# A cross-attention kernel on one core: an order planned from both ends, and a set-up laid out anew

## The chip, the cores and the metric

The kernel runs on one core of one Trainium2 chip. The metric is the time of one execution on the device in microseconds (us), as a median of several runs. TensorE (PE) multiplies matrices, VectorE (DVE), ScalarE (ACT) and GpSimd (POOL) work elementwise, and SyncE (SP) issues DMAs, which ACT and POOL can do as well.

## What is computed

32 samples of x and of a context y, each of 256 channels by 1024 positions, in float32. For each sample:

```python
x_q = jnp.einsum('oc,bcn->bno', w_qk, y)
x_k = jnp.einsum('oc,bcn->bon', w_qk, x)
x_v = jnp.einsum('oc,bcn->bon', w_v, x) + b_v[None, :, None]
energy = jnp.einsum('bnc,bcm->bnm', x_q, x_k)
attention = jax.nn.softmax(energy, axis=-1)
attention = attention / (1e-07 + attention.sum(axis=1, keepdims=True))
x_r = jnp.einsum('bcn,bnm->bcm', x_v, attention)
x_r = jax.nn.relu(jnp.einsum('oc,bcn->bon', w_t, x - x_r) + b_t[None, :, None])
return x + x_r
```

So each sample has a 1024 by 1024 energy, a softmax over its rows, a division by the sums of its columns, and products with small weights before and after.

## The kernel before

**Three forms.** To multiply float32 values fast, each operand is kept as three forms (high, rest, low), and each product is the sum of three. `load_y` (L277) and `load_x` (L308) make the forms of y and x: ACT casts the high one, POOL or an accumulating DMA makes the other two. The weights are folded first: `gw` from w_qk squared, `vw` from w_t and w_v, `tw` from w_t transposed.

**Work of a sample.** Tokens name it: `k` the keys gf = gw x (`keys`, L363), `v`/`V` the values uf, `W` the straight product tw x, whose evictions ACT writes to xe with a bias, `E0` to `E7` eight row tiles of 128 rows of the energy (`energy`, L402), `A0` to `A7` their products with the values (`attention`), `S` the column sums, `O` the finish, `X`/`Y` the loads of x and y for what comes next. A `^` takes one of two upper pairs of PSUM banks (`high_pair`, L771), which alternate, 3 first; the others take a lower pair. `A` writes pair 2 for channels c=0 and pair 3 for c=1, so `O` has to read both before the upper pairs serve again.

**A row tile.** After the 12 products of a tile, DVE takes the row minimum, ACT the exponential, DVE a reciprocal, ACT writes the high form of each half, DVE the rest form and then adds the half to the column sums `acc`. All of these read the tile's two banks, and the tile that is next to use them waits until the last one is through. ACT and POOL make the low form.

**Who sets the order.** Every operation is first registered with the planner (`Plan`, L17) with an engine, a duration, a lag and the names that it reads and writes. PE keeps the order of the tokens (strings at L124 to L138: SET_UP, FIRST for sample 0, STEADY, BEFORE, LAST). `Plan.order` (L60) gives each operation a due time, counted back from its followers without regard to how busy the engines are, and then runs a list schedule: an engine that comes free takes the operation with the earliest due time among those that can start within a small look-ahead. `emit` (L113) tries three look-aheads, and the order with the shortest planned span is written out. For the planner an operation that reads a bank waits for readers of it on other engines that are registered ahead of it. On the chip each engine then runs its own list strictly in that order, waiting for data by semaphore. The planner lets a DVE operation whose operands lie in SBUF (`dve_in_sbuf`, L206) wait for a POOL operation that has begun; it makes POOL wait only behind such a wait.

**Set-up.** Loads go out on SP and ACT (L606 to L616): two of w_qk, four of x's first sample, one each of w_t and w_v, then y, b_v (spread over 128 partitions) and b_t on SP. `first_x` (L663) makes the first forms of x in four pieces (two halves of 512 columns, two channel blocks k): of six products of forms that DVE and POOL make, POOL makes the rest form of k=1, DVE that of k=0 and all four low ones. `first_keys` (L693) multiplies a form by gw, four products of a token being two; token `fL10` is the low form of k=1, half 0. `turn_w` transposes w_t; ACT copies it to wtT, and POOL makes the first step (`twd`) of its low form. `biases` (L736) multiplies w_t by b_v on DVE, sums it and makes three small biases. `load_y(0, direct=True)` lets POOL subtract y's high form from y in one piece of 1024 columns per partition; an accumulating DMA adds that to the low form.

Of the kernel before, what the change touches and what calls it, by code (L numbers as in the profile page):

```python
# [9 lines left out]
F32 = mybir.dt.float32  # L10
# [6 lines left out]
class Plan:  # L17
# [7 lines left out]
    SEEN = 0.1  # L25

# [33 lines left out]
    def order(self):  # L60
        ops = self.ops
        behind, before, last = {}, {}, None
        for op in ops:
            op.feeds = []
        for op in ops:
            for other in op.needs.values():
                other.feeds.append(op)
            if op.engine == "pe":
                if last is not None:
                    behind[last.at], before[op.at] = op, last  # L70
                last = op
        for op in reversed(ops):
            due = [f.due - op.busy - op.lag - self.SEEN for f in op.feeds]
            if op.at in behind:
                due.append(behind[op.at].due - op.busy)
            op.due = min(due, default=0.0) - op.early
        left = [len(op.needs) + (op.at in before) for op in ops]
        can = [0.0] * len(ops)
        free, ready, held, out = {}, {}, 0.0, []
        for op in ops:  # L80
# [3 lines left out]
        while len(out) < len(ops):  # L84
# [18 lines left out]
            if op.at in behind:  # L103
                nexts.append((behind[op.at], t + busy))
# [8 lines left out]
    def emit(self):  # L113
# [13 lines left out]
FIRST = (  # L127
    "V0^ W0^ V1 E0 E1^ W1 E2 E3 A0 A1 E4 E5 A2 A3 E6 E7 S X A4 A5 k0 Y2 A6 k1 A7 v0 Y3 O"
# [13 lines left out]
def kernel(  # L142
# [29 lines left out]
    Y_ON_POOL = False  # L172
# [83 lines left out]
    wtb = one.tile([P, KC], F32, name="wtb")  # L256
# [20 lines left out]
    def load_y(q, direct=False):  # L277
# [3 lines left out]
        name = {j: f"yf{s}{j}" for j in ORDER}  # L281
        from_ = y[b].rearrange("(k p) n -> p k n", p=P)[:, :, ts(half, MB)]
        by_sync(7.0 if b else 3.5, ["xr01", "xr11"] if b == 0 else [], ["yr"], lambda: sync.dma_start(r, from_))
        on_act(N, ["yr"], [name[HIGH]], lambda: act.copy(f[:, HIGH], r))
        if direct:
            on_pool(
                N, ["yr", name[HIGH]], [name[REST]],
                lambda: pool.tensor_tensor(f[:, REST], r, value(f[:, HIGH]), ALU.subtract),
            )
        else:  # L290
            on_act(N, [name[HIGH]], [name[REST]], lambda: act.mul(f[:, REST], value(f[:, HIGH]), -1.0))
            by_pool(9.0, [name[REST]], [name[REST]], lambda: accumulate(f[:, REST], from_))
        on_act(N, [name[HIGH]], [name[LOW]], lambda: act.mul(f[:, LOW], value(f[:, HIGH]), 1.0 / UP))
        if direct and q == 0 and Y_ON_POOL:
            on_pool(
                N, [name[LOW], name[REST]], [name[LOW]],
                lambda: pool.tensor_tensor(f[:, LOW], value(f[:, LOW]), value(f[:, REST]), ALU.add),
            )
        else:
            by_pool(  # L300
                8.0, [name[LOW], name[REST]], [name[LOW]],
                lambda: accumulate(value(f[:, LOW]), value(f[:, REST])),
            )
# [546 lines left out]
```

## Time and profile before

| | us |
|---|---|
| median of 3 runs (1948.5 to 1950.74) | 1948.7 |
| the profiled execution's own time | 1950.96 |
| its span, first to last instruction | 1949.2 |
| PE busy | 1938.1 (99%) |
| DVE busy | 1553.4 (80%) |
| ACT busy | 1434.6 (74%) |
| POOL busy | 1252.9 (64%) |

The span is what the profiler saw between the first and the last instruction; the execution's own time has 1.76 us around it. A line of the profile names the engine, the operation, the tile written and those read, the shape, and in brackets the idle time before it with what ended it. All operations go through one helper, so their line number is L188 throughout, and the tiles tell them apart.

### The profile page before, as it was taken

Reading aid. Unit: us, or ns where it says so; the run is one execution under the profiler, and the core shown is the slowest. Engines: PE = TensorE matmul, PEld = TensorE weight load, DVE = VectorE, ACT = ScalarE, POOL = GpSimd, SP = SyncE. Lnnn points to the kernel's source line nnn. Section 1 sums busy time; section 2 is a strip of 40 time slices with the busy share of each in tenths; the row PEclk is TensorE's granted clock in tenths of the full one; section 3 lists DMA queues with packets and bytes.
Section 4 is the critical chain, followed back from the end, with each engine's and each line's share of the span. In section 5 each row is a group of like instructions: output and inputs, shape, how many; then the busy total and the mean of one; then the engine's idle time right before and its main releaser. Section 6 shows DMA issues by size and latency. Waiting matters only on the chain.

```text
span 1949.2 us, 25297 instructions
## 1 busy us (share of the span) xinstructions
PE 1938.1 (99%) x9252; PEld 1632.4 (84%) x9252; DVE 1553.4 (80%) x2173; ACT 1434.6 (74%) x1863; POOL 1252.9 (64%) x645
## 2 busy tenths in 40 slices
PE   8999999999999999999999999999999999999998
PEld 7888888888888888888888888888888888888887
DVE  7887887877887778878788887887877887778887
ACT  6678776787767877667877678776787767877765
POOL 4577665766656666566766577665766656666564
PEclk9999999999999999999999999999999999999999
DMA  5545545564455554455544555545564445554540
GB/s 145 123 119 141 125 112 110 120 149 121 115 103 129 140 129 118 110 126 124 139 118 106 125 119 141 125 111 110 119 150 121 115 103 129 141 125 121 111 98 33
DMA packets 82140, 234.81 MB, mean 120 GB/s; under 512 B 7521, under 2 KB 8673, under 8 KB 82017
## 3 DMA queue, kind: packets, MB, share of 16 engines
q0 software_dynamic: 35280, 99.10, 29.7%
q1 hardware_dynamic: 46032, 133.19, 20.3%
q8 instruction: 73, 1.20, 0.2%
q10 hardware_dynamic: 704, 0.92, 0.1%
q14 instruction: 51, 0.41, 0.1%
HBM read 133.56 MB, written 33.55 MB: 86 GB/s over the span
## 4 chain that ended last, share of the span: by engine, by line
PE 98%; DVE 1%; ACT 0%; DMA 0%; issue 0%; POOL 0%; ACTq 0%
PE banks L188 98%; DVE xf L188 0%; DMA xr<-in_x_dram 0%; DVE ef L188 0%; DVE acc L188 0%; ACT xf L188 0%; ACT ef L188 0%; DVE z L188 0%; ACT banks L188 0%; DVE small L188 0%; POOL xf L188 0%; ACT xe L188 0%; DVE banks L188 0%; ACTq L188 0%; DVE gw L188 0%
## 5 line engine op out<-in xcount | busy, mean ns | idle before, releaser
L188 POOL TENSOR_TENSOR ef<-ef 128x1024 fp32r<-128x1024 f32 x256 | 614.6, 2407 | 442.2 <-ACT ef L188 229.4
L188 PE MATMUL banks<-gf,yf 128*128 128x512 f32 x3072 | 727.9, 389 | 0.4 <-DVE acc L188 0.4
L188 PE MATMUL banks<-ef,uf 128*128 128x512 f32 x3072 | 722.5, 389 | 1.2 <-DVE acc L188 1.2
L188 PEld LDWEIGHTS banks<-ef,uf 128*128 128x128 f32 x3072 | 576.5, 188 | 121.6 <-DVE acc L188 1.1
L188 PEld LDWEIGHTS banks<-gf,yf 128*128 128x128 f32 x3072 | 574.3, 188 | 119.5 <-ACT ef L188 0.8
L188 DVE SCALAR_TENSOR_TENSOR ef<-banks,small,ef 128x512 fp32r<-128x512 f32 x512 | 379.1, 746 | 149.5 <-ACT ef L188 149.2
L188 DVE TENSOR_REDUCE small<-banks 128x1 f32<-128x1024 f32 x256 | 312.6, 1221 | 102.7 <-PE banks L188 100.7
L188 ACT ACTIVATE banks<-banks,small 128x1024 f32<-128x1024 f32 x256 | 276.7, 1081 | 138.8 <-DVE small L188 138.1
L188 ACT ACTIVATE ef<-banks,small 128x512 fp32r<-128x512 f32 x512 | 320.7, 690 | 38.2 <-DVE small L188 38.2
L188 DVE SCALAR_TENSOR_TENSOR acc<-banks,small,acc 128x512 f32<-128x512 f32 x448 | 329.9, 742 | 0.0
L188 POOL TENSOR_TENSOR z<-z,xe 128x1024 f32<-128x1024 f32 (+1 forms) x64 | 151.3, 2381 | 205.0 <-DVE z L188 205.0
L188 ACT ACTIVATE ef<-ef 128x1024 fp32r<-128x1024 f32 x256 | 268.9, 1069 | 12.8 <-ACT ef L188 0.7
L188 ACT ACTIVATE gf<-banks 128x1024 fp32r<-128x1024 f32 x64 | 65.1, 1019 | 184.8 <-PE banks L188 184.7
L188 PEld LDWEIGHTS banks<-vw,xf 128*128 128x128 f32 x1536 | 193.8, 193 | 5.0
L188 PE MATMUL banks<-vw,xf 128*128 128x256 f32 x1536 | 195.2, 284 | 0.0
L188 PE MATMUL banks<-xf,gw 128*128 128x512 f32 x768 | 186.4, 391 | 4.0 <-DVE xf L188 2.3
L188 PE MATMUL banks<-xf,tw 128*128 128x512 f32 (+1 forms) x774 | 185.8, 389 | 0.8 <-DVE z L188 0.6
L188 PEld LDWEIGHTS banks<-xf,gw 128*128 128x128 f32 x768 | 143.9, 188 | 35.3 <-DVE xf L188 3.2
L188 PEld LDWEIGHTS banks<-xf,tw 128*128 128x128 f32 x774 | 142.5, 188 | 29.5 <-DVE z L188 0.8
L188 POOL TENSOR_TENSOR z<-z,xo 128x1024 f32<-128x1024 f32 x62 | 158.3, 2553 | 4.7 <-ACT ef L188 4.6
L188 POOL TENSOR_TENSOR xf<-xr,xf 128x1024 fp32r<-128x1024 f32 (+1 forms) x64 | 151.0, 2381 | 7.3 <-DVE xf L188 6.1
L188 DVE RECIPROCAL small<-small 128x1 f32<-128x1 f32 x256 | 41.1, 161 | 116.1 <-ACT banks L188 114.8
(65 smaller groups left out, 1403.7 us busy)
## 6 DMA issues: line engine op xcount, KB each, us to landing
yr<-in_ctx_dram SPq DMA_DIRECT2D x64, 512.0 KB, 3.7
yf<-yf POOLq DMA_DIRECT2D x64, 512.0 KB, 4.6
yf<-in_ctx_dram POOLq DMA_DIRECT2D x63, 512.0 KB, 6.7
xo<-in_x_dram SPq DMA_DIRECT2D x62, 512.0 KB, 4.5
xr<-in_x_dram SPq DMA_DIRECT2D x62, 512.0 KB, 3.4
xf<-xf POOLq DMA_DIRECT2D x62, 512.0 KB, 6.5
out_dram<-z SPq DMA_DIRECT2D x62, 512.0 KB, 5.0
out_dram<-z SPq DMA_DIRECT2D x3, 256.0 KB, 2.1
```

The lines of the kernel that those rows point to most:

```text
L188: self.last = getattr(self.engine, name)(*args, **kwargs)
```

## The change

- **The planner.** Due times of the first turn are counted as before. In three further turns they come from a second list schedule that runs from the end to the start and gives every engine one operation at a time, the later start of the turn before going first; the forward schedule then runs again. An engine takes what can start now, unless something more urgent becomes ready while that would run and is later than PE's own lateness allows; then it waits for that one. Of the four orders the one with the shortest planned span is written out.
- **Loads.** The planned landings are new (x 6.0 and 7.4 us where they were 3.8 and 5.0, for instance). w_t and w_v are loaded in two halves each, one on SP and one on ACT; ten loads now stand ahead of y, b_v and b_t.
- **Value bias.** w_t times b_v becomes four products of one column on PE (token `b`, ahead of `fR11` and `Q`), written to a corner of bank 7. DVE keeps the three small operations. b_v is now loaded as two columns in 4-byte pieces, as b_t is.
- **y's first forms in two pieces.** For the first half of y the first 256 positions (512 columns per partition) get both the rest and the low form on POOL; the other 256 positions get theirs by accumulating DMAs, as all later y do.
- **Column sums** are registered ahead of the high form of the same half, in every tile; for the planner ACT's high form then comes behind DVE's sum.
- **Token order.** SET_UP and FIRST are new; STEADY, BEFORE and LAST stay. FIRST has four `^` tokens where it had three.

```diff
--- before.py
+++ after.py
+    LOOKS = (0.0, 0.3, -0.6, 0.0)
...
+    def from_the_end(self):
+        left = [len(op.feeds) + (op.next is not None) for op in self.ops]
...
+        while todo:
...
+            op = max((o for o in ready[engine] if can[o.at] <= now), key=lambda o: (o.start, o.at))
+            ready[engine].remove(op)
+            todo -= 1
+            free[engine] = over = now + op.busy
+            op.due = -over - op.early
...
+        behind = -min(op.due for op in ops)
...
-            within = start + self.LOOK
-            op = min((o for o in ready[engine] if can[o.at] <= within), key=lambda o: (o.due, o.at))
+            op = min((o for o in ready[engine] if can[o.at] <= start), key=lambda o: (o.due, o.at))
+            late = start + op.busy - behind - self.LOOK
+            soon = [o for o in ready[engine] if can[o.at] < start + op.busy and o.due < min(op.due, late)]
+            if soon:
+                op = min(soon, key=lambda o: (o.due, o.at))
...
+            if engine == "pe":
+                behind = t - op.due
...
+    def best(self):
+        self.link()
         best = None
-        for look in (0.0, 0.15, 0.3):
-            self.LOOK = look
+        for turn, self.LOOK in enumerate(self.LOOKS):
+            if turn:
+                self.from_the_end()
             out = self.order()
             if best is None or self.span < best[0]:
-                best = self.span, out
-        self.span, out = best
-        for op in out:
+                best = self.span, [(op, op.start) for op in out]
+        return best
+
...
 SET_UP = (
-    "G x0 fH10 b fH00 fR10 x1 T fH01 fL10 Q fH11 y fR01 fL01 fL00 fR00 fL11 fR11"
+    "x0 G fR10 x1 fH10 T fR01 y fL10 fL00 fH00 b fR11 Q fL11 fR00 fL01 fH11 fH01"
 )
 FIRST = (
-    "V0^ W0^ V1 E0 E1^ W1 E2 E3 A0 A1 E4 E5 A2 A3 E6 E7 S X A4 A5 k0 Y2 A6 k1 A7 v0 Y3 O"
+    "V1^ V0^ W1 E0 E1^ W0^ X E2 E3 A0 A1 E4 E5 A2 Y2 A3 E6 E7 A4 A5 k0 k1 A6 S A7 Y3 O v0"
 )
...
-    def load_y(q, direct=False):
+    NQ = 2
+    QB = MB // NQ
+
...
+        by_sync(7.0 if q else 7.8, [], ["yr"], lambda: sync.dma_start(r, from_))
+        on_act(N, ["yr"], y_names(s, HIGH), lambda: act.copy(f[:, HIGH], r))
...
+            if q == 0 and which[0] == 0:
+                on_pool(
+                    columns, ["yr"] + nh, nr,
+                    lambda: pool.tensor_tensor(third, r[:, :, at], value(high), ALU.subtract),
+                )
+                on_act(columns, nh, nl, lambda: act.mul(low, value(high), 1.0 / UP))
+                on_pool(columns, nl + nr, nl, lambda: pool.tensor_tensor(low, value(low), value(third), ALU.add))
+                return
+            on_act(columns, nh, nr, lambda: act.mul(third, value(high), -1.0))
+            by_pool(9.0, nr, nr, lambda: accumulate(third, from_[:, :, at]))
+            on_act(columns, nh, nl, lambda: act.mul(low, value(high), 1.0 / UP))
+            by_pool(8.0, nl + nr, nl, lambda: accumulate(value(low), value(third)))
+
+        for which in ([0], [1]) if q == 0 else ([0, 1],):
+            pieces(which)
...
-            on_pe(KC, MB, [f"yf{s}{j}"] + [f"gf{j}{k}" for k in range(KC)], [at[h]], of)
+            on_pe(KC, MB, [f"yf{s}{j}{n % HT * NQ // HT}"] + [f"gf{j}{k}" for k in range(KC)], [at[h]], of)
...
         def halves(h):
             ph, to, a = both[:, h], f[:, :, ts(h, MB)], acc[:, ts(h, MB)]
             high, rest = names[HIGH][h], names[REST][h]
+            if n == 0:
+                on_dve(MB, [at[h], nm[2]], [f"acc{h}"], lambda: dve.tensor_scalar(a, ph, ri, None, ALU.mult))
+            else:
+                on_dve(
+                    MB, [at[h], nm[2], f"acc{h}"], [f"acc{h}"],
+                    lambda: dve.scalar_tensor_tensor(a, ph, ri, a, ALU.mult, ALU.add),
+                )
             on_act(MB, [at[h], nm[2]], [high], lambda: act.mul(to[:, HIGH], ph, ri))
             on_dve(
                 MB, [at[h], nm[2], high], [rest],
@@ -429,13 +484,6 @@
                     to[:, REST], ph, ri, value(to[:, HIGH]), ALU.mult, ALU.subtract
                 ),
             )
...
-    bv = two(3)[:, 1]
+    bv = two(3)[:, 0, P + KC : P + 2 * KC].rearrange("p (k o) -> p k o", o=1)
...
-    by_sync(5.6, [], ["wt"], lambda: sync.dma_start(wt, w_t.rearrange("(k p) c -> p k c", p=P)), early=25.0)
-    by_act(5.6, [], ["wv"], lambda: act.dma_start(wv, w_v.rearrange("(k p) c -> p k c", p=P)), early=25.0)
+    load(["wqk0", "wqk1"], 2.7, [(wqk[:, k], w_qk[ts(k, P)]) for k in range(KC)])
+    load(["xr00", "xr10"], 6.0, [(xr[:, k, half[0]], x[0, ts(k, P), half[0]]) for k in range(KC)])
+    load(["xr01", "xr11"], 7.4, [(xr[:, k, half[1]], x[0, ts(k, P), half[1]]) for k in range(KC)])
+    load(["wt0", "wt1"], 8.3, [(wt[:, k], w_t[ts(k, P)]) for k in range(KC)])
+    load(["wv0", "wv1"], 9.2, [(wv[:, k], w_v[ts(k, P)]) for k in range(KC)])
...
     def biases():
-        by_sync(4.0, ["xr01", "xr11"], ["bv"], lambda: sync.dma_start(bv, b_v.rearrange("(o c) -> o c", o=1).to_broadcast([P, C])))
-        by_sync(4.0, ["xr01", "xr11"], ["bt"], lambda: sync.dma_start(bt, b_t.rearrange("(k p o) -> p k o", p=P, o=1)))
-        product = work[:, N + KC * C :].rearrange("p (k c) -> p k c", k=KC)
+        by_sync(6.8, [], ["bv"], lambda: sync.dma_start(bv, b_v.rearrange("(k p o) -> p k o", p=P, o=1)))
+        by_sync(6.8, [], ["bt"], lambda: sync.dma_start(bt, b_t.rearrange("(k p o) -> p k o", p=P, o=1)))
+        wtb = banks[:, 7, C : C + KC]
+
+        def product():
+            for i in range(KC):
+                for k in range(KC):
+                    matmul(
+                        wtb[:, i : i + 1], wtT[:, k * C + i * P : k * C + (i + 1) * P], bv[:, k], k == 0, k == KC - 1
+                    )
+
+        plan.add("pe", 0.45, 0.163, ["wtT", "bv", "z1", "acc0", "acc1"], ["wtb", "bank7"], product)
 
         def of():
-            dve.tensor_tensor(product, wt, bv.unsqueeze(1).to_broadcast([P, KC, C]), ALU.mult)
-            dve.tensor_reduce(wtb, product, AX.X, ALU.add)
             dve.tensor_scalar(ubias[:, :, 0], wtb, EPS, None, ALU.mult)
-            dve.tensor_tensor(xbias[:, :, 0], bt[:, :, 0], wtb, ALU.subtract)
-            dve.tensor_scalar(nbias[:, :, 0], xbias[:, :, 0], -1.0, None, ALU.mult)
-
-        plan.add("dve", 2.0, 0.0, ["wt", "bv", "bt", "z1", "xe1"], ["bias"], of)
+            dve.tensor_tensor(nbias[:, :, 0], wtb, bt[:, :, 0], ALU.subtract)
+            dve.tensor_scalar(xbias[:, :, 0], nbias[:, :, 0], -1.0, None, ALU.mult)
+
+        plan.add("dve", 0.6, 0.0, ["wtb", "bank7", "bt", "z1"], ["bias"], of)
...
-            load_y(0, direct=True)
+            load_y(0)
             load_y(1)
```

## Rows read from the trace of the kernel before

**Rows 1.** The page: span, and each engine's busy time, share, instructions.
```profile
span 1949.2 us, 25297 instructions
...
PE 1938.1 (99%) x9252; PEld 1632.4 (84%) x9252; DVE 1553.4 (80%) x2173; ACT 1434.6 (74%) x1863; POOL 1252.9 (64%) x645
```
**Rows 2.** Busy time by stretch: stretch, its us, engines' busy us, TensorE's granted clock, DMA.
```profile
0.00:16.56 16.56, 11.46 (x47) 8.52 (x47) 9.62 (x13) 7.73 (x13) 8.61 (x12) 1.00 0.46 150
16.56:48.44 31.88, 31.49 (x152) 26.46 (x153) 25.47 (x37) 24.36 (x33) 13.46 (x8) 0.95 0.56 140
18.02:21.40 3.38, 3.38 (x15) 3.13 (x14) 3.28 (x8) 2.66 (x4) 1.59 (x1) 0.50 0.99 263
...
100.00:1880.00 1780.00, 1780.00 (x8505) 1501.47 (x8504) 1419.26 (x1983) 1331.38 (x1724) 1166.93 (x595) 1.00 0.52 123
1898.60:1906.40 7.80, 6.64 (x29) 4.67 (x27) 7.76 (x13) 6.83 (x10) 5.36 (x3) 1.00 0.26 106
```
**Rows 3.** PE's waits, whole run: waiter, releaser, total us, times, longest.
```profile
PE banks L188 <- DVE xf L188: 2.3, 2, 2.0
...
PE banks L188 <- DVE acc L188: 1.5, 3, 0.8
```
**Rows 4.** Timeline of PE, set-up and first sample: start us, us, what, idle before.
```profile
9.29 0.61 PE L188 MATMUL banks<-z 128*128 128x128 f32 x4
...
16.56 2.58 PE L188 MATMUL banks<-xf,gw 128*128 128x512 f32 x8 [2.03 <-DVE xf L188]
18.93 4.14 PE L188 MATMUL banks<-vw,xf 128*128 128x256 f32 x24
...
25.65 3.04 PE L188 MATMUL banks<-vw,xf 128*128 128x256 f32 x24
...
28.52 5.63 PE L188 MATMUL banks<-gf,yf 128*128 128x512 f32 x24
```
**Rows 5.** Timeline of DVE in the set-up.
```profile
9.68 1.78 DVE L188 TENSOR_TENSOR xf<-xr,xf 128x512 fp32r<-128x512 f32 x1
11.38 0.41 DVE L188 SCALAR_TENSOR_TENSOR gw<-banks,gw 128x256 fp32r<-128x256 f32 x1
...
13.06 4.04 DVE L188 SCALAR_TENSOR_TENSOR xf<-xf 128x512 fp32r<-128x512 f32 x3
...
18.60 0.68 DVE L188 TENSOR_TENSOR xe<-z 128x512 f32<-128x512 f32 x1
19.31 0.69 DVE L188 TENSOR_REDUCE wtb<-xe 128x2 f32<-128x512 f32 x1
```
**Rows 6.** Timeline of POOL in the set-up.
```profile
9.29 1.62 POOL L188 TENSOR_TENSOR xf<-xr,xf 128x512 fp32r<-128x512 f32 x1
11.25 1.34 POOL L188 TENSOR_TENSOR xe<-acc,tw 128x512 f32<-128x512 f32 x1 [0.34 <-ACT tw L188]
13.14 2.82 POOL L188 TENSOR_TENSOR yf<-yr,yf 128x1024 fp32r<-128x1024 f32 x1 [0.55 <-ACT yf L188]
```
**Rows 7.** Waits of SP's queue, first 20 us.
```profile
SPq L188 <- DMA xr<-in_x_dram: 1.9, 1, 1.9
...
SPq L188 <- DMA z<-in_L_xattn_w_qk_dram: 0.9, 1, 0.9
```
**Rows 8.** Timeline of SP: issue of b_t's load.
```profile
6.85 0.37 SPq L188 DMA_DIRECT2D z<-in_L_xattn_b_t_dram  x1
```
**Rows 9.** DMA issues of the page: count, KB each, median us to landing.
```profile
z<-in_L_xattn_b_t_dram SPq DMA_DIRECT2D x1, 1.0 KB, 4.5
```
**Rows 10.** DVE's waits, whole run.
```profile
DVE ef L188 <- ACT ef L188: 149.2, 186, 1.5
```
**Rows 11.** Timeline of sample 15's end and sample 16's start, DVE and PE.
```profile
984.25 2.48 DVE L188 SCALAR_TENSOR_TENSOR z<-banks,ubias,rc 128x1024 f32<-128x1024 f32 x2
...
986.64 1.21 DVE L188 SCALAR_TENSOR_TENSOR gf<-gf,banks 128x1024 fp32r<-128x1024 f32 x1
...
987.10 1.09 PE L188 MATMUL banks<-xf,tw 128*128 128x512 f32 x4
```

More of the change, by code (lines that the diff above doesn't have):

```diff
@@ L58, in add, with link @@
         self.ops.append(op)
[L60 to L65, printed above, removed]
+    def link(self):
+        last = None
+        for op in self.ops:
+            op.feeds, op.next, op.before = [], None, None
             for other in op.needs.values():
@@ L69, in order @@
                 if last is not None:
[L70 removed]
+                    last.next, op.before = op, last
                 last = op
[L72 removed]
+        for op in reversed(self.ops):
             due = [f.due - op.busy - op.lag - self.SEEN for f in op.feeds]
[L74 to L75 removed]
+            if op.next is not None:
+                due.append(op.next.due - op.busy)
             op.due = min(due, default=0.0) - op.early
[L77 removed]
+    def from_the_end(self):
+        left = [len(op.feeds) + (op.next is not None) for op in self.ops]
+        can = [0.0] * len(self.ops)
+        free, ready, todo = {}, {}, len(self.ops)
+        for op in self.ops:
+            free.setdefault(op.engine, 0.0)
+            if not left[op.at]:
+                can[op.at] = op.lag
+                ready.setdefault(op.engine, []).append(op)
+        while todo:
+            now, engine = min(
+                (max(free[e], min(can[op.at] for op in some)), e) for e, some in ready.items() if some
+            )
[4 more added lines that the diff above has]
+            op.due = -over - op.early
+            befores = [(o, over + o.lag + self.SEEN) for o in op.needs.values()]
+            if op.before is not None:
+                befores.append((op.before, over))
+            for o, when in befores:
+                can[o.at] = max(can[o.at], when)
+                left[o.at] -= 1
+                if not left[o.at]:
+                    ready.setdefault(o.engine, []).append(o)
+    def order(self):
+        ops = self.ops
+        left = [len(op.needs) + (op.before is not None) for op in ops]
         can = [0.0] * len(ops)
         free, ready, held, out = {}, {}, 0.0, []
+        behind = -min(op.due for op in ops)
         for op in ops:
@@ L102, in order @@
             nexts = [(f, t + done + self.SEEN) for f in op.feeds]
-            if op.at in behind:
-                nexts.append((behind[op.at], t + busy))
+            if op.next is not None:
+                nexts.append((op.next, t + busy))
             for f, when in nexts:
@@ new lines, in load_y, with pieces @@
+        on_act(N, ["yr"], y_names(s, HIGH), lambda: act.copy(f[:, HIGH], r))
+        def pieces(which):
+            at = slice(which[0] * QB, (which[-1] + 1) * QB)
+            high, low, third = (f[:, j, :, at] for j in range(FORMS))
+            nh, nl, nr = (y_names(s, j, which) for j in range(FORMS))
+            columns = KC * QB * len(which)
+            if q == 0 and which[0] == 0:
[10 more added lines that the diff above has]
+            by_pool(8.0, nl + nr, nl, lambda: accumulate(value(low), value(third)))
```

57 lines of the change are left out of this document (16 added, 41 removed).

## The prediction

> **What bounds the kernel now.** I read the busy times by stretch first, then PE's waits, then the timelines of the stretches in which PE is not full. The page shows PE busy for 1938.1 of 1949.2 us [rows 1], and the stretch from 100 to 1880 us shows it busy for 1780.00 of 1780.00 [rows 2]. There nothing can be gained by a better order on the other engines: the number of products stays the same. What is left lies at the two ends. The set-up up to 16.56 us has PE busy for 11.46 us [rows 2]; the rest of sample 0, up to 48.44, loses 0.39 us; and a stretch near the end, 1898.60 to 1906.40, loses 1.16 [rows 2]. The waits agree: two for DVE's forms of x, 2.3 us, and three for the column sums, 1.5 us [rows 3].
>
> A second loss doesn't show as idle time. From 18.02 to 21.40 us TensorE's granted clock was 0.50, that is 1.2 GHz, against 1.00 (2.4 GHz) up to 16.56 and from 100 on [rows 2]. It fell after PE had waited 2.03 us for a form of x and had worked only since 16.56 [rows 4]. The same 24 products of the values took 4.14 us at 18.93 and 3.04 at 25.65 [rows 4], so it cost 1.1 us there, and some 0.4 in the two products of the keys ahead of them.
>
> So the change can move the set-up, sample 0 and the last sample by some microseconds each, or break the full stretch in the middle.
>
> **Set-up: the forms of x.** The last keys wait for DVE: three low forms took 4.04 us from 13.06, to 17.10, and PE's last eight products of the keys began in between, at 16.56, and ended where the values begin, 18.93 [rows 4, 5]. A DVE operation of that shape takes 0.68 us when POOL is still (18.60), but the one at 9.68 took 1.78 [rows 5], and POOL's subtraction of 9.29 ended at 10.91, 0.55 before it [rows 6]. In the same way the forms from 13.06 lasted until POOL's long subtraction of y (13.14, 2.82 us, to 15.96) was over, and a little more: 4.04 - 3 x 0.68 = 2.0 us of waiting. Conversely POOL's 1.62 at 9.29 is 0.28 above the 1.34 at 11.25 [rows 6]. In these rows the two take turns, one operation each.
>
> The Trainium skill, "SBUF — State Buffer", section "Who interferes with whom", says the same: a DVE instruction with two SBUF inputs and a GpSimd one that reads SBUF exclude each other for a whole instruction. That speaks against this change, whose planner makes POOL wait only in one case, and which gives POOL one operation more; rival B works it out from the rows.
>
> The sum, as a shift of DVE's last form from 17.10: the 2.0 us behind the long subtraction go; of the new half-size pieces (half of 1024 columns, at the 1.34 of the same shape [rows 6]) I let one get between DVE's forms, +1.34; the weight step at 11.38 moves to the idle time ahead of x's landing, now that the planner knows it, -0.41 [rows 5]. That is 17.10 - 2.0 + 1.34 - 0.41 = 16.0. In the new token order five tokens (`fL11`, `fR00`, `fL01`, `fH11`, `fH01`), ten products, stand from the last low form of k=1 on, at 5.63 / 24 = 0.235 us each [rows 4]: 2.35, so 18.4, and I put 0.2 for the handovers between the engines: 18.6, against 18.93. Gain 0.3. `b` and `Q` stand ahead of them and are covered by the wait for that form; without this cover PE would lose up to the 0.61 us of `b` (below).
>
> The clock: the wait ahead of the last products gets shorter and the products ahead of it denser, so I take it not to fall there: gain 1.1 [rows 4]; the 0.4 lies within the 18.93. The other end is that it falls as before: nothing. Together the set-up gains 1.4.
>
> **Loads.** SP's queue waited 0.9 us for w_qk and 1.9 us for x, which its next loads don't read [rows 7]. Those were y's, the ninth load, and b_t's, the eleventh. I read it so that a load waits for the one eight places ahead of it. With ten loads in front, the three for b_v, b_t and y come eleventh to thirteenth and wait for x's pieces, the earliest where b_t's went out, 6.85 us [rows 8]. y's goes later by the time between the two landings; the others on SP behind it wait for its readers anyway. y's high form is ACT's, in order, so a late y also holds what ACT has behind it (among it w_t's high form, for which POOL's `twd` waits). The first energy at 28.52 is far enough away. b_v lands 4.5 us after its issue if it is like b_t [rows 9], at 11.4, or a microsecond or more later if it is third.
>
> **Value bias.** DVE loses 0.68 + 0.69 = 1.37 us [rows 5]; they lay at 18.60, ahead of the last forms of the keys, while PE had nine microseconds of other work, so they bring nothing to the end. PE gets four small products; the nearest row is the four transposes, 0.61 us for 128 columns each [rows 4], and with one column they can't be dearer: between 0 and 0.61, of which I take 0.5, under the cover named above. The new wait for b_v holds `fR11`, `Q` and all later PE work; by 12.8, when `fL00` can be done, it should be over; if b_v comes third it is just so (12.8 is an estimate: 14.1 of rival B, below, less one POOL operation). DVE's small bias operations now wait for PE, with the steps of vw queued behind them: up to 0.5 us, which I put at nothing, since `V1^` waits for the keys as well.
>
> **y in pieces.** The first half's low form no longer needs a DMA; the second piece has two DMAs in a chain, but E2 is the first to read it, over five microseconds after E0, since the tiles E0 and E1 alone take 5.63 [rows 4]. Nothing either way.
>
> **Sums ahead of high forms.** DVE waited 149.2 us in 186 places for ACT's high form [rows 10], 0.8 us each. A sum now fills each such gap. In the middle PE is full and it brings nothing. In sample 0 it shortens the release of a tile's banks: I take 0.3 of the 0.39 us lost there. In the last sample PE lost 1.16 us to the release of E1's banks; there DVE had put the next tile's row minimum ahead of E1's rest forms. Against that stands a side effect of FIRST's fourth `^`: the upper pairs change roles in all later samples. E1^ of the last sample now lies in pair 2, which A0 writes first, so two more products (0.47 us) have to come behind the release. I take 0.5 gained; the ends are 1.16 gained and 0.47 lost.
>
> **Sum.** 1.4 + 0.3 + 0.5 = 2.2 us. The profiled execution would go from 1950.96 to 1948.8. It is 2.3 above the median, with a span of 1949.2, so the shift is what carries over: 1948.7 - 2.2 = 1946.5.
>
> **Rivals.**
>
> *A, the set-up runs as planned.* If POOL's pieces don't get between DVE's forms (because y is late and POOL idles), PE itself is the bound: from its first product, which needs x (6.85), DVE's cast (some 0.4) and POOL's rest form (1.34) [rows 6, 8], at 8.6 us, it has 24 products of 0.235, eight squares of 256 columns (some 1.9, as 0.235 for 512), transposes and bias (0.61 and 0.5), 8.7 us, to 17.3: 1.6 earlier. With the clock (1.1) and nearly all of the losses of sample 0 and the end (0.4 and 1.1) that is 4.2: 1944.5. For it: the planned landings now agree with the trace. Against it: the turns that DVE and POOL take.
>
> *B, the turns of rows 5 and 6 eat the gain.* If `twd` and both pieces of y are ready on POOL while DVE has forms left, each of these waits 1.34 us. Then DVE's last form is at 17.10 - 2.0 - 0.41 + 2 x 1.34 = 17.4 (`twd` was in the way before too), and the form for `fL00` is late as well, so that `b`, `fR11`, `Q` and the ten products follow in a row. DVE's fourth form after POOL's first would end at 8.6 + 4 x 0.55 + 0.6 + 2 x 1.34 = 14.1 (0.6 for POOL's small cast). From there 0.9 for `fL00` and `fH00`, then 0.5 + 0.5 + 1.9 + 2.35 make 6.1, to 20.2, 1.3 behind 18.93. PE's gaps ahead of that are as long as before, so the clock falls as well. With 0.8 gained elsewhere: 1949.2.
>
> *C, slower: the full stretch breaks.* Because the upper pairs change roles, W1^ of every sample from the second on now writes pair 3, which the second of O's two operations frees. These ran from 984.25 to 986.73, and W1^ began at 987.10 [rows 11]: 0.37 us of room where the other pair had 1.6. If the new order puts one gf form (1.21 us at 986.64 [rows 11]) ahead of the second, PE loses 0.84 us in each of 30 samples, 25 us: 1974. It decides from 0.37 us of extra DVE work on. Against it: the planner sees this dependence, can turn the two round, and the sums now start earlier.
>
> *D, nothing.* The first of four turns still uses the old due times; if it wins, the middle stays, and if the set-up's gains and losses cancel, it is 1948.7.
>
> **How the numbers follow.** Forecast 0.42, A 0.23, B 0.20, C 0.08, D 0.07. The predicted time is the forecast's, 1946.5. The low end takes in A with all of the losses at the end gone and a little of its bound (1943.2), the high end B with nothing gained elsewhere and b_v's wait (1950.8); only C lies outside, and a little of A. About 0.2%, 3.9 us, is what a measurement of this kernel can tell from no change: 1944.8 and 1952.6. Faster than that are most of A and a few of the forecast, 0.24; slower is C and a little of B, 0.10; the same 0.66.
>
> **What would show it.** PE's first energy product: 27.1 us in the forecast, 25.8 in A, 29.8 in B. In the set-up, DVE forms of x above 1 us and POOL operations above 1.4 show the turns; y's load at 6.85 or later shows the waiting of the eleventh load. The granted clock should stay at 1.00 up to the end. PE's waits for DVE's forms of x should fall below 2.3 us in B's absence, those for column sums below 1.5. From 100 to 1880 PE should be busy all the time; a repeated wait ahead of xf,tw would be C. I am wrong if that stretch has gaps, if the last sample loses more than before, or if the keys end before 17 us.

## The result, and the profile after

The changed kernel takes 1954.45 us (median; 1953.6 to 1957.06) against 1950.74 (1948.5 to 1951.5) for the kernel before beside it: a ratio of 1.0025, 95% interval 1.0015 to 1.0035 (the ratios here and below are those on record; the two medians alone give 1.0019). It is slower, and above the predicted range. The profiled execution took 1953.6 us with a span of 1951.65, against 1950.96 and 1949.18; the 2.47 us between these spans are what the traces can account for. Executions of one kernel differ by 1 to 6 us, and one of f4's below, of 6142.96 us, is left out, since the record shows no cause for it.

The page of the changed kernel, and its busy time by stretch (columns as in [rows 2]):

```profile
span 1951.7 us, 25256 instructions
...
PE 1939.0 (99%) x9260; PEld 1634.7 (84%) x9260; DVE 1567.1 (80%) x2171; ACT 1428.2 (73%) x1865; POOL 1255.8 (64%) x647
```
```profile
0.00:16.56 16.56, 12.56 (x45) 10.41 (x46) 7.96 (x15) 7.00 (x12) 6.75 (x12) 0.79 0.73 228
8.18:15.01 6.83, 6.10 (x16) 4.82 (x17) 5.12 (x5) 3.25 (x6) 3.91 (x4) 0.50 0.72 209
...
100.00:1880.00 1780.00, 1780.00 (x8505) 1501.52 (x8504) 1432.37 (x1982) 1325.06 (x1726) 1167.51 (x595) 1.00 0.51 122
```

The middle is as full as in [rows 2]. The difference lies at the two ends, as predicted, but with the other sign. PE's waits, answering [rows 3], then its timeline, answering [rows 4]:

```profile
PE banks L230 <- POOL xf L230: 2.9, 1, 2.9
PE banks L230 <- DVE xf L230: 1.9, 1, 1.9
PE banks L230 <- DVE ef L230: 1.5, 2, 1.3
```
```profile
8.91 2.07 PE L230 MATMUL banks<-xf,gw 128*128 128x512 f32 x4 [2.94 <-POOL xf L230]
...
15.03 0.95 PE L230 MATMUL banks<-z,acc 128*128 128x1 f32 x8
...
20.16 2.60 PE L230 MATMUL banks<-xf,gw 128*128 128x512 f32 x10 [1.87 <-DVE xf L230]
22.59 5.91 PE L230 MATMUL banks<-vw,xf 128*128 128x256 f32 x48
...
31.09 5.60 PE L230 MATMUL banks<-gf,yf 128*128 128x512 f32 x24
...
50.14 2.20 PE L230 MATMUL banks<-gf,yf 128*128 128x512 f32 x9
```

The first energy product stands at 31.09 instead of 28.52: the set-up loses 2.57. From it to the fifth energy tile it is 19.05 instead of 19.92: sample 0 gains 0.87. At the end the span stretches 0.84 further past the last product. With 0.07 gained elsewhere, 2.57 - 0.87 - 0.07 + 0.84 = 2.47.

Where the set-up loses is seen on DVE and POOL, answering [rows 5, 6]:

```profile
7.09 0.42 DVE L230 CAST xf<-xr 128x512 fp32r<-128x512 f32 x1
...
10.34 2.96 DVE L230 SCALAR_TENSOR_TENSOR xf<-xf 128x512 fp32r<-128x512 f32 x3
16.10 0.16 DVE L230 TENSOR_SCALAR ubias<-banks 128x2 f32<-128x2 f32 x1 [2.80 <-PE banks L230]
...
16.36 3.15 DVE L230 TENSOR_SCALAR xbias<-nbias 128x2 f32<-128x2 f32 x1
19.43 0.68 DVE L230 SCALAR_TENSOR_TENSOR xf<-xf 128x512 fp32r<-128x512 f32 x1
```
```profile
7.59 1.26 POOL L230 TENSOR_TENSOR xf<-xr,xf 128x512 fp32r<-128x512 f32 x1 [6.28 <-DVE xf L230]
8.80 1.07 POOL L230 CAST xf<-xr 128x512 fp32r<-128x512 f32 x1
...
14.38 1.35 POOL L230 DMA_DIRECT2D yf<-in_ctx_dram  x1 [2.84 <-ACT yf L230]
15.30 1.75 POOL L230 TENSOR_TENSOR yf<-yr,yf 128x512 fp32r<-128x512 f32 x1
16.54 1.73 POOL L230 TENSOR_TENSOR xe<-acc,tw 128x512 f32<-128x512 f32 x1
17.76 1.71 POOL L230 TENSOR_TENSOR yf<-yf 128x512 fp32r<-128x512 f32 x1
```

DVE is in order. Three low forms of x are done at 13.30, the fourth stands behind the bias operations, and these wait 2.80 us for PE's product. Then `xbias`, two columns from SBUF to SBUF, takes 3.15 us: it stands from 16.36 and is over when POOL's third operation in a row is (17.76 + 1.71 = 19.47). Only then comes the fourth low form, and PE, which has waited 1.87 us, gets its last ten key products. This suggests theory Q: **an SBUF operation of DVE that comes while POOL runs its operations back to back is kept out until the run is over**. Its rival, theory C: the low clock from 8.18 to 15.01, in a stretch that begins while PE waits for its first rest form of x, is what makes the set-up late.

### The profile page after: what moved, and what is told of

Read it like the earlier page. It is cut to its first block, busy times and chain, and to the rows that moved or that the text cites. A ratio compares the mean times of both kernels' runs of the same rounds, so it can differ in the third digit from the quotient of the medians.

```text
span 1951.7 us, 25256 instructions
## 1 busy us (share of the span) xinstructions
PE 1939.0 (99%) x9260; PEld 1634.7 (84%) x9260; DVE 1567.1 (80%) x2171; ACT 1428.2 (73%) x1865; POOL 1255.8 (64%) x647
## 3 DMA queue, kind: packets, MB, share of 16 engines
q0 software_dynamic: 35680, 99.10, 29.2%
## 4 chain that ended last, share of the span: by engine, by line
PE 99%; DVE 1%; ACT 0%; POOL 0%; issue 0%; DVEq 0%
PE banks L230 99%; DVE xbias L230 0%; DVE ef L230 0%; DVE z L230 0%; DVE acc L230 0%; ACT ef L230 0%; POOL xf L230 0%; DVE small L230 0%; DVE xf L230 0%; ACT banks L230 0%; DVE banks L230 0%; DVE xe L230 0%; DVEq L905 0%; ACT gw L230 0%; DVE gw L230 0%
## 5 line engine op out<-in xcount | busy, mean ns | idle before, releaser
L230 POOL TENSOR_TENSOR ef<-ef 128x1024 fp32r<-128x1024 f32 x256 | 638.2, 2499 | 368.6 <-ACT ef L230 197.1
L230 DVE SCALAR_TENSOR_TENSOR ef<-banks,small,ef 128x512 fp32r<-128x512 f32 x512 | 368.6, 745 | 52.9 <-ACT ef L230 52.6
L230 ACT ACTIVATE ef<-banks,small 128x512 fp32r<-128x512 f32 x512 | 331.9, 687 | 76.2 <-DVE acc L230 68.6
L230 DVE SCALAR_TENSOR_TENSOR acc<-banks,small,acc 128x512 f32<-128x512 f32 x448 | 320.6, 745 | 5.5
L230 POOL TENSOR_TENSOR z<-z,xo 128x1024 f32<-128x1024 f32 x62 | 149.0, 2403 | 144.4 <-DMA xo<-in_x_dram 129.8
```

The costliest lines, as they stand in the source:

```text
L230: self.last = getattr(self.engine, name)(*args, **kwargs)
```

## The experiments

All stand against runs of the kernel before on the same chip. The first four take one cause each.

**e1** reads `xbias` from PSUM:
```diff
-            dve.tensor_scalar(xbias[:, :, 0], nbias[:, :, 0], -1.0, None, ALU.mult)
+            dve.tensor_tensor(xbias[:, :, 0], bt[:, :, 0], wtb, ALU.subtract)
```
**e2** leaves that and moves the three bias operations behind the fourth low form in the planned order:
```diff
...
+        out.remove(self.later)
+        out.insert(out.index(self.low11) + 1, self.later)
...
```
**e3** puts 24 products of zeros between the squares of w_qk and the first key product, **e4** is e2 and e3 together:
```diff
...
+                lambda: [pe.matmul(banks[:, 7, :P], few, few, start=True, stop=True) for _ in range(24)],
...
```


> The kernel after, with xbias taken straight from PSUM (b_t minus the product) and not from nbias in SBUF; the order of all engines is the same. Theory Q (DVE's queue): in the set-up the last x form waits behind the three small bias operations, of which xbias took 3.15 us beside POOL's work, so it starts about 3 us earlier, and PE, whose squares end at 18.3, waits no longer than 0.7 us for it instead of 1.87: the first energy product at 29.2 to 30.0 us instead of 31.09, the time 1.1 to 1.9 us below the kernel after. Theory C (clock): what counts is TensorE at 1.2 GHz from 8.18 to 15.0 us; this edit does not touch it and gives less than 1 us.

> The kernel after, with the three bias operations written out behind DVE's last x form and not ahead of it; nothing else moves. Theory Q: DVE neither waits 2.80 us for PE nor 3.15 us beside POOL ahead of that form; it ends near 13.3 us, PE does not wait for it at all, the first energy product comes at 29.2 us, the time falls by 1.9 us against the kernel after. Theory C: same clock record as after (0.5 for about two of the short stretches), the remaining 0.7 us at that product over the kernel before is the clock's.

> The kernel after, with 24 products of zeros on PE between the squares of w_qk and the first product of the keys, where PE waited 2.94 us; their results are overwritten and nothing else moves. Theory C: TensorE is granted 1.00 through the set-up, the bias products come about 1.5 to 2 us earlier than 15.03, and the first energy product moves from 31.09 to 27.4 to 29.5 us, more than e2 gives; the time falls by 2 to 3.5 us. Theory Q: PE comes earlier to the bias products but the last x form still stands behind xbias, which waits for POOL; less than 1.5 us.

> e2 and e3 together. If both theories carry a part, the first energy product comes at 27.0 to 27.6 us (PE full from 8.9 us but for DVE's forms), 3.5 to 4 us below the kernel after and 1 us below the kernel before at that point; the time about 1950 or below. If the two are the same loss seen twice, it is no better than the better of e2 and e3.

Measured: e1 1955.18, ratio 1.0028 (1.0017 to 1.0038); e2 1952.49, 1.0014 (1.0005 to 1.0023); e3 1956.04, 1.0035 (1.0022 to 1.0048); e4 1954.94, 1.0025 (1.0015 to 1.0035). DVE of e1, then of e2:

```profile
15.87 0.15 DVE L230 TENSOR_TENSOR xbias<-z,banks 128x2 f32<-128x2 f32 x1
15.93 4.95 DVE L230 SCALAR_TENSOR_TENSOR xf<-xf 128x512 fp32r<-128x512 f32 x1
```
```profile
11.57 3.56 DVE L233 SCALAR_TENSOR_TENSOR xf<-xf 128x512 fp32r<-128x512 f32 x4
...
16.54 3.83 DVE L233 TENSOR_SCALAR xbias<-nbias 128x2 f32<-128x2 f32 x1
```

The wait isn't a property of `xbias`. Read from PSUM it takes 0.15 us, and the next SBUF operation, the low form, takes 4.95 instead of 0.68. In e2 the low forms are out of POOL's way, `xbias` waits 3.83, and the steps of vw behind it hold the values by 0.92 us; the first energy product stands at 30.27, not at the 29.2 that I had expected. What I expected of e1, a gain, was wrong: I had moved the first victim only. e4 loses e2's gain in the same way (`xbias` 4.71). e3 speaks against C. Its clock was 1.00 from the first key product to the wait, but the zeros were twice as many instructions as meant (48 in 5.52 us), and the time saved was given back as waiting:

```profile
12.09 1.17 PE L230 MATMUL banks<-xf,gw 128*128 128x512 f32 x4
...
22.02 3.65 PE L230 MATMUL banks<-xf,gw 128*128 128x512 f32 x10 [3.38 <-DVE xf L230]
```

A low clock was not free everywhere, though. Where it fell behind a wait, PE was full and paid. In e1 the granted clock was 0.50 from 20.01 to 26.83, and the ten key products took 4.64 us and the 48 of the values 6.58 (in e9 below, at 1.00, they take 2.63 and 5.92). With the longer wait, and a first key product 0.84 later (9.75), this puts e1's first energy product at 34.52, 3.43 later than in the changed kernel:

```profile
20.93 4.64 PE L230 MATMUL banks<-xf,gw 128*128 128x512 f32 x10 [3.02 <-DVE xf L230]
```

**e5** joins e1's and e2's edits, so that DVE has no SBUF operation left between the forms of x and vw, and puts the end's 512-column piece, DVE's operation and store, ahead of the 256-column one. **e6** is e5 with 11 products of zeros. **e7** puts the whole set-up of before back (tokens, loads, bias on DVE, y in one piece), **e8** puts e5's tokens in the order of before, `b` behind `T`.

> The changed kernel with three orders mended: the two-column bias operations behind the last x form on VectorE, the last of them read from PSUM instead of SBUF, and at the very end the finished 512-column piece ahead of the 256-column one. Theory Q (an SBUF operation of VectorE that GpSimd's back-to-back tensor operations keep out): no SBUF operation is left on VectorE between the x forms and the steps of vw, so the values start when the key products end (20.6, not 21.66 with the biases moved alone) and the first energy product stands at 29.2 to 29.4, against 30.27 there and 31.09 in the changed kernel. The end of 0.84 us is VectorE's order: from the last product to the end of the span 3.7, not 4.49. Time 1950.8 to 1951.2, ratio about 1.0009. Theory C (the half clock is what costs): the clock at 1.2 GHz lasts as long as in the changed kernel, the first energy product stays at 30.3 or later. A rival for the end: the last two stores are slow by themselves, and 4.4 stays.

> The same, and 11 products of zeros, 22 instructions on TensorE, put between the squares of w_qk and the first key product, where the changed kernel's TensorE is idle for 2.94 us. Theory C: the granted clock stays at 1.00 to the values, from the first key product to the last 8.8 us as in the kernel with both edits before (12.38 to 21.21), so with the first at 9.0 to 9.9 the last ends at 17.8 to 18.7 and the first energy product stands at 26.5 to 27.5; time 1948.0 to 1949.0, ratio below 1. Theory Q alone: the key products wait for x forms, whatever the clock, the first energy product stays within 0.4 of the one without the extra products.

> The changed kernel with the whole set-up of before put back: token order, loads, the value bias's product on VectorE and the first y in one piece with its low form by DMA. What is left of the change is the planner, sample 0's order and the column sums ahead of the high forms. If the set-up carries the loss, the first energy product comes back to 28.5 (28 to 29), sample 0 keeps its gain (first to fifth energy tile 19.05, not 19.92), the end keeps its loss of 0.84: time 1948.7 less 0.9 plus 0.8, the ratio within 0.0005 of 1. If the planner's new due times carry it, the key products wait for the last x form here too, the first energy product stands at 30 or later and the ratio is 1.001 or more.

> The kernel with three orders mended, and the set-up's tokens in the order of before (high form of k=1 first; the biases behind the turning of w_t, which they now need). The difference from the three mends alone is the order of the tokens. If the wait of 2.94 us for GpSimd's rest form, put first, is the step that failed, the first key product stands at 7.4 to 7.9 instead of 8.9 to 10.1, the clock does not fall before 9, and the first energy product comes 1 us or more earlier than without this edit: 28 or earlier. If TensorE only waits for the same rest form one product later, it stands within 0.4 of the one without.

Measured: e5 1951.05, 1.0004 (0.9994 to 1.0014); e6 1950.21, 1.0006 (0.9997 to 1.0016); e7 1949.99, 0.9999 (0.9990 to 1.0009); e8 1954.3, 1.0022 (1.0012 to 1.0031). e5 did a little more than Q says: the values start at 20.37, the first energy product stands at 28.87. e7 places the loss: with the old set-up it stands at 28.64, sample 0 keeps its gain (to the fifth tile 19.04), and the end its loss in part (4.23 from the last product to the end of the span; 3.65 before, 4.49 in the changed kernel). e8 missed: the first key product did come at 8.20, but all forms came earlier, and POOL's run with them, so the last low form was caught (3.83 us) and PE waited 2.00 for the bias operations behind it. The first energy product of e5, then of e7 (both rows cut off at 32 us):

```profile
28.87 3.34 PE L238 MATMUL banks<-gf,yf 128*128 128x512 f32 x14
```
```profile
28.64 3.56 PE L231 MATMUL banks<-gf,yf 128*128 128x512 f32 x15
```

e6 points to a race within one program: whether DVE's last low form begins before POOL's run. Its times were 1949.69 to 1951.5 in eight executions, of which there is no trace, and 1955.22 and 1955.39 in two, one of them the profiled one. DVE, then POOL:

```profile
11.20 8.39 DVE L238 SCALAR_TENSOR_TENSOR xf<-xf 128x512 fp32r<-128x512 f32 x4
```
```profile
13.94 1.35 POOL L238 DMA_DIRECT2D yf<-in_ctx_dram  x1 [1.53 <-ACT yf L238]
14.85 1.75 POOL L238 TENSOR_TENSOR yf<-yr,yf 128x512 fp32r<-128x512 f32 x1
16.09 1.73 POOL L238 TENSOR_TENSOR xe<-acc,tw 128x512 f32<-128x512 f32 x1
17.31 1.72 POOL L238 TENSOR_TENSOR yf<-yf 128x512 fp32r<-128x512 f32 x1
```

The fourth of these low forms began at 14.1 and took 5.50 us. In e5 it began at 14.4, POOL's run at 15.40, and it took 0.68.

If Q holds, keeping POOL back must cure the changed kernel with no order touched. **e9** adds one instruction to it: POOL copies a column of DVE's last low form before it turns to y and w_t.
```diff
...
+                plan.ops[-1].look = lambda: pool.tensor_copy(rc[:, :1], value(low[:, MB - 1 :]))
```
**e10** is e6 with this hold, **e11** e7 with it and the end's order of e5, **b2** the kernel before with the hold alone.

> The changed kernel with one instruction more: GpSimd copies one column of the last x form made on VectorE, and so begins y's and w_t's operations only when VectorE is done with x. No order of any engine is changed. Theory Q (GpSimd's back-to-back run keeps VectorE's SBUF operations out): the two-column bias operation takes 0.15 to 0.3 us instead of 3.15 and the last x form 0.68, TensorE's wait of 1.87 us for it goes, the first energy product stands at 29.0 to 29.5 instead of 31.09, time 1951.5 to 1952.7. Rival (the two columns are slow by themselves, or VectorE waits for something else): the bias operation stays at 3 us, the first energy product at 31 or later. Second rival: y's forms, begun some 2 us later, become what the first energy product waits for, which then shows a wait of its own.

> The three mended orders, the 11 products of zeros, and GpSimd held until the last x form. Theory Q: the last x form takes 0.68 us in every execution, where without the hold the profiled one took 5.50; all times lie together at 1949 to 1950, the first energy product stands at 26.8 to 28.0. Theory C adds: the granted clock stays at 1.00 from the first key product to the values. Rival: GpSimd's later start delays y, and TensorE waits ahead of the first energy product.

> The changed kernel with the whole set-up of before, GpSimd held until the last x form, and the end's 512-column piece ahead of the 256-column one. Theory Q: the low forms of x, which took 4.54 us for two beside GpSimd's operations, take 0.7 to 1.7 each, TensorE's wait of 2.05 us for them goes, and with it the fall of the clock: the first energy product stands at 26.0 to 27.0, against 28.64 without the hold; with 0.4 at the end the time is 1947.0 to 1948.0, ratio about 0.9987. Rival: y in one piece, begun later on GpSimd, is what the first energy product then waits for; no gain.

> The kernel before with the hold alone. Theory Q: VectorE's three low forms of x, 4.04 us, take 2.0 to 3.2, TensorE's wait of 2.03 us for the last of them goes or is cut to under 0.5, the clock does not fall at 18, and the first energy product stands at 26 to 27 instead of 28.52; time 2 us less, ratio 0.999. Rival: GpSimd's operation for w_t and y come 1 to 2 us later, and a wait for one of them takes the place of the wait for x: ratio 1.000.

Measured: e9 1950.72, 1.0002 (0.9993 to 1.0012); e10 1950.03, 1.0000 (0.9991 to 1.0009); e11 1951.87, 1.0008 (0.9999 to 1.0018); b2 1950.02, 0.9999 (0.9990 to 1.0009). DVE and POOL of e9:

```profile
16.47 0.17 DVE L252 TENSOR_SCALAR xbias<-nbias 128x2 f32<-128x2 f32 x1
16.55 0.68 DVE L252 SCALAR_TENSOR_TENSOR xf<-xf 128x512 fp32r<-128x512 f32 x1
```
```profile
17.30 0.19 POOL L252 COPY rc<-xf 128x1 f32<-128x1 f32 x1 [4.45 <-DVE xf L252]
```

0.17 us instead of 3.15, and the low form at once: it was POOL's operations that kept DVE out, as Q says (what in a run does it is taken up in the last section). The first energy product stands at 29.03, and from 1.0025 to 1.0002 the hold gives back nearly all of the loss, though POOL turns to y at 17.55 instead of 14.38. In e10, e6 with the hold, none of ten executions took more than 1951.09. C falls as the cause with e9 and e10 (which also has the mended orders and the zeros) side by side, from the first key product to the first value:

```profile
10.21:20.53 10.32, 10.32 (x45) 8.42 (x45) 6.98 (x13) 5.22 (x10) 5.72 (x6) 0.83 0.51 163
```
```profile
8.65:18.90 10.25, 9.20 (x44) 7.29 (x45) 6.91 (x13) 5.48 (x11) 7.68 (x7) 1.00 0.75 205
```

At a clock of 0.83 PE was busy all the time, at 1.00 it waited for forms of x, and the stretch took 10.3 us either way. Here the low clock filled waiting time.

In b2 the rival that I had named came true. The keys ended at 15.60 instead of 19.14, at a clock of 1.00, and nothing came of it. y, now behind the hold, and w_t's rest form were what PE met next:

```profile
20.16 2.56 PE L209 MATMUL banks<-xf,tw 128*128 128x512 f32 x10 [1.21 <-POOL tw L209]
...
28.45 4.83 PE L209 MATMUL banks<-gf,yf 128*128 128x512 f32 x20 [1.55 <-DMA yf<-yf]
```

e11 missed as well (I had expected 1947.0 to 1948.0). Its keys ended at 16.00, but the next load of y could go out only at 18.98, when POOL had read the first one from the same tile. ACT stood 5.00 us waiting for it with a form of the values behind, DVE's last form of the keys queued behind that one, and PE waited 3.44 us for it.

The changed kernel has the cure for y, its first half made without a DMA. So the last four join b2's quick keys with the change's parts. **f1** is the changed kernel with the tokens (`b` last) and loads of before, `xbias` from PSUM, the hold, and at the end the 512-column piece's DVE operation and its store each moved ahead of the 256-column one's. **f2** is f1 with the bias product back on DVE, **f3** f1 with y in one piece, **f4** f1 without the hold.

> The changed kernel with the token order and the loads of before, the value bias's product on TensorE behind the key products (its last two-column operation read from PSUM), GpSimd held until the last x form, and at the end VectorE's operation and the store of the 512-column piece each ahead of that of the 256-column piece. If y's landing is what the faster key products ran into, then with the first half of y made on the chip the key products end at 15.5 to 16.5, the values follow without a wait, and the first energy product stands at 24.5 to 26, against 28.52 before; sample 0 keeps 19.05 between first and fifth energy tile; from the last product to the end 3.7 instead of 4.1. Time 3.5 to 4.5 us below before, ratio 0.9977 to 0.9985. Rival: the second half of y, by DMA behind GpSimd's later start, makes the third or fifth energy tile wait, and half of the gain is given back.

> The same with the value bias's product on VectorE, as before. If that product holds up the key forms, which stand behind it on VectorE, the first energy product comes later than in the kernel with the product on TensorE, by the 2.9 to 4 us that VectorE spends on it beside GpSimd, less what the values cover: 25 to 27. If the key forms have room behind the values, no difference above 0.5 us.

> The kernel with both edits, its first y back in one piece with the low form by DMA. If y's landing is the limit, the first energy product or its low products wait as in the two kernels held before, and stand at 28 or the sample loses the same 2 to 3 us inside its first energy tile; time 2.5 to 3.5 us above the kernel with two pieces. If y is not the limit: the same time.

> The kernel with both edits, without the hold on GpSimd. Theory Q: GpSimd's w_t and y operations run while VectorE still has low forms of x to make; one of these takes 2 to 5 us instead of 0.68, TensorE waits 2 us or more for it, the clock falls, and the first energy product stands 2 to 4 us later than with the hold. If the hold is worth nothing, within 0.4 us.

Measured, before at 1950.35: **f1 1946.59, 0.9982 (0.9973 to 0.9991); f2 1945.79, 0.9979 (0.9970 to 0.9988)**; f3 1947.79, 0.9993 (0.9984 to 1.0002); f4 1949.33 (1949.58 if the execution of 6142.96 us is counted), 0.9996 (0.9987 to 1.0005). PE of f1, of f2, of f3 and of f4:

```profile
6.75 1.23 PE L257 MATMUL banks<-xf,gw 128*128 128x512 f32 x4 [0.47 <-ACT gw L257]
...
15.09 0.95 PE L257 MATMUL banks<-z,acc 128*128 128x1 f32 x8
15.89 6.01 PE L257 MATMUL banks<-vw,xf 128*128 128x256 f32 x48
...
24.49 5.60 PE L257 MATMUL banks<-gf,yf 128*128 128x512 f32 x24
```
```profile
6.38 1.24 PE L257 MATMUL banks<-xf,gw 128*128 128x512 f32 x4 [0.47 <-ACT gw L257]
...
14.71 5.92 PE L257 MATMUL banks<-vw,xf 128*128 128x256 f32 x48
...
23.21 5.60 PE L257 MATMUL banks<-gf,yf 128*128 128x512 f32 x24
```
```profile
28.52 4.83 PE L258 MATMUL banks<-gf,yf 128*128 128x512 f32 x20 [2.21 <-DMA yf<-yf]
```
```profile
16.18 3.69 PE L236 MATMUL banks<-xf,gw 128*128 128x512 f32 x8 [2.04 <-DVE xf L236]
```

Each part now has a price. The hold: 2.7 us by the medians (f4 - f1); in the traces the stretch from the first key product to the values is 13.40 against 9.14, through the wait of 2.04 and a clock of 0.50 behind it, from 16.22 to 19.63. y in two pieces: 1.2 by the medians (f3 - f1), where I had expected 2.5 to 3.5, and a wait of 2.21 in the trace. The bias product on PE costs: f2 is 0.8 faster than f1, and that stretch is 8.33 against 9.14. My expectation of f2 was wrong; the planner put DVE's product at 27.27, behind the key forms, where it holds up nothing. The end: 3.63 us after the last product in f1, 4.10 in e5, whose order on DVE is the same but whose first store stands behind a later one. So e5's order gives back some 0.4 of the 0.84, and moving the store by itself the rest; the split is rough, since e7, with the changed kernel's order, stands at 4.23. f1 and f2 beat both kernels; f2, about 4 us below before, is the one to keep.

## Why the prediction was wrong

- **The step that failed** is "In these rows the two take turns, one operation each". In [rows 6] each POOL operation has ended before the next begins, so these rows could not tell taking turns from waiting for the end of POOL's run. In the set-up's early rows of the changed kernel turns are still what is seen (DVE's two rest forms from 7.83 take 2.58); later POOL's whole run went through first. Where the sum has +1.34 for one POOL operation between DVE's, `xbias` alone was kept out until the run's end and took 3.15. The Trainium skill, "SBUF — State Buffer", section "Who interferes with whom", says that issue order decides who blocks, and for a whole instruction. The trace agrees for the POOL operation that had begun at 15.30, ahead of `xbias` at 16.36. It differs for the two behind it: they began at 16.54 and 17.76, later than `xbias`, and went first all the same.
- **"up to 0.5 us, which I put at nothing"**, of DVE's bias operations waiting for PE: DVE waited 2.80 there. I named the steps of vw as queued behind them and missed the fourth low form of x, which PE waited for. The planner's order was not worked through to that row.
- **The product itself**: 0.95 us (0.95 also at a clock of 1.00, in f1), above my upper bound of 0.61. I argued that one column can't be dearer than 128; the row shows x8 where the transposes show x4, two instructions for each product. f1 and f2 price the move at 0.8 us lost.
- **The weight step moved ahead of x's landing, -0.41**: it turned round. x's first half landed earlier than before (6.14 against 6.83), but DVE's cast stood behind three weight steps, began at 7.09, and POOL's rest form, asked for first in the new order, ended at 8.85; PE's first key product came at 8.91 (7.43 before). In f1 the loads and order of before gave 6.75, with x landing at 5.78.
- **The clock**, "I take it not to fall there": it fell, but sooner, from 8.18 on (1.2 GHz), in PE's first wait. There it cost little, as e10 shows; the 1.1 us at the values were gained (48 products in 5.91 us where [rows 4] have 4.14 and 3.04), and the waits lost more. Nor could these 1.1 us be counted from a median of 1948.7. Of the 33 executions of before beside f1, the 13 with a mean granted clock of 1.000 took 1948.42 to 1949.59, the 20 at 0.999 took 1949.33 to 1951.23; the traced one, with the fall, had 0.998 and took 1950.96. So 1948.7 seems to be the time without the fall; no trace of such an execution was kept.
- **Sample 0**: 0.87 gained instead of 0.3; e7 keeps it without the new set-up. DVE's wait for ACT's high forms fell from 149.2 us [rows 10] to 52.6. **The last sample**: nothing instead of 0.5. The release of the banks moved from DVE's sums to its rest forms, and PE's wait from the attention products [rows 2, 3] to an energy tile (0.40 and 0.75 us became 1.28 and 0.24). These waits are longer in sum, 1.52 against 1.15, which I had named as a sign of being wrong:

```profile
1904.16 3.02 PE L230 MATMUL banks<-gf,yf 128*128 128x512 f32 x12 [1.28 <-DVE ef L230]
...
1907.65 4.60 PE L230 MATMUL banks<-ef,uf 128*128 128x512 f32 x19 [0.24 <-DVE ef L230]
```

- **Not foreseen**: the last 4 us. The planner put a 256-column piece that PE hadn't done ahead of the ready 512-column one, and DVE stood still:

```profile
1945.65 1.14 DVE L230 SCALAR_TENSOR_TENSOR z<-banks,nbias,xr 128x256 f32<-128x256 f32 x2 [0.53 <-PE banks L230]
```

The second operation in that row is the 512-column one.

- **Rivals.** The prediction's C (the full stretch breaks; not theory C above) did not happen. B had POOL's operations as the cause and the sign for the set-up: 29.8 for the first energy product, 31.09 measured. Its terms were turns of 1.34 each, where the run cost 3.15 on top of DVE's 2.80. What held: the middle, the loads waiting for the one eight places ahead (w_v's, the ninth, at 3.21, after w_qk had landed; y's at 6.15 and not 6.85, since x landed sooner), "Nothing either way" for y in pieces as the kernel stands.

## What to carry to other kernels

Before giving GpSimd more, list every SBUF operation that VectorE issues while GpSimd's run lasts, and make GpSimd wait for the last one that TensorE needs: one column copied was worth 2.7 us in f1. Work through the queue of each in-order engine behind a new wait to the operation that the critical engine wants, however small the waiting instruction is. And after each cure look for what stands next: quick keys were worth nothing until y's landing was cured too.

## What the hardware showed that I had not expected

- VectorE's SBUF operations of 0.17 to 0.68 us took 3.15 to 5.50 beside a run of GpSimd operations. In such a run these begin 1.22 to 1.26 us apart and last 1.71 to 1.78 each, so the next has begun well before the former ends (16.54 against 17.05). How long before goes with who is let in. In the set-ups of all 18 traces a waiting VectorE operation with no operand in PSUM met the border of two overlapping GpSimd operations (DMA issues among them) 32 times: it got in at all 12 where the overlap was 0.10 us or less (8.80 against 8.86 in the changed kernel; in e8 16.97 against 17.07, which ended the wait of 3.83 there), and at none of the 20 where it was 0.26 or more. That the overlap decides is an inference, not tested alone. In e6 the run that kept it out began with a GpSimd DMA issue (13.94); whether that alone does it is open. POOL of e8:

```profile
16.97 1.79 POOL L238 TENSOR_TENSOR yf<-yf 128x512 fp32r<-128x512 f32 x1
```

- The squares of w_qk took 2.35 us in e10 and 3.71 in e9, the same instructions: the granted clock is on record as 1.00 from 4.16 on in one and from 7.07 on in the other. The first key product moves with the squares. How much of the spread between executions of one kernel this makes is open, since each kernel has one trace.
- Products of fp32 with 128 or one column show as two instructions each: 48 for 24 in e3, 8 for four in the bias product. The four transposes of w_t show as four.
